# A transformer block in float32 on one core: the share of bands whose fourth convolution block runs on TensorE goes from 9 of 20 to 7 of 16, a norm group's two statistics become one step, and the order is computed anew

## The chip, the cores and the metric

The kernel runs on one core of a Trainium2 chip. The metric is device time in microseconds of one execution; the time before is the median of three runs. PE is TensorE, DVE is VectorE, ACT is ScalarE, POOL is GpSimd and SP is SyncE, which here only issues DMAs.

## The reference

For 16 images of 128 channels and 96x96 pixels, in float32 throughout: a norm over the channels of each pixel, channel attention with eight heads and a residual; a second norm, a feed-forward part of 512 hidden channels (1x1 in, 3x3 depthwise, exact GELU, 1x1 out) and a second residual.

```python
xn1 = _layernorm(x_hwc, ln1_w, ln1_b)
attn_out = _attention(xn1, wq, wk, wv, wp)
x = x + attn_out.transpose(0, 3, 1, 2)
xn2 = _layernorm(x_hwc, ln2_w, ln2_b).transpose(0, 3, 1, 2)
x = x + _ffn(xn2, w_in, w_dw, w_out)
# _attention: q, k normalised over the pixels; softmax(q k^T * scale) is 16x16 for each head
# _ffn:
h1 = jnp.einsum('bchw,oc->bohw', xn_nchw, w_in[:, :, 0, 0])
h2 = lax.conv_general_dilated(h1, w_dw, ..., padding=((1, 1), (1, 1)), feature_group_count=HID)
h3 = jax.nn.gelu(h2, approximate=False)
return jnp.einsum('bchw,oc->bohw', h3, w_out[:, :, 0, 0])
```

## The kernel before

**Tiling.** Channels lie on the 128 partitions. An image is cut into six *bands* of 16 rows (96 bands in all), a band into four *units* of 4 rows (384 pixels). The 512 hidden channels are four *blocks* of 128.

**The norms.** Each norm works on groups of 512 pixels, 18 to an image (288 groups for each norm, 576 in all). `forth` (L662) transposes the group on PE into one of two PSUM banks (`pT_a`, `pT_b` for the first and second norm), so that a pixel's channels lie along a row. `stats` (L669) takes the statistics on DVE, two instructions of 256 elements for a group. POOL makes the variance (`ve`, L676) and its power -1/2 (`rstd`, L680); for the second norm DVE makes one small vector (`nb`, L684). ACT scales the group out of PSUM (`zT`, L716 and L720), and PE transposes it back (`pB`, L767), whence ACT places it in a ring of rows in SBUF (`xn`, L771, L773). In the first norm PE also accumulates a Gram matrix from `zT` (L730), from which the attention is worked out.

**The feed-forward part.** For a band and a block, a *job*: PE multiplies by the input weights (`hidden`, L942, four matmuls), ACT copies the result into a padded buffer `h1` of the block (`kept`, L945). Of the nine taps of the 3x3 convolution, the centre and six others are taken on DVE (`tap`, L970): six instructions of some 1,520 elements, which accumulate in place in one `h3` buffer, the first from the centre row, each later one onto what the one before it wrote. The last two taps are products on ACT (`products`, L963), which two DMAs from POOL's queue add on (L977). ACT then applies GELU (L981). A job of the fourth block can be done by PE instead: `by_matmuls` (L1035) takes nine matmuls for each unit, 36 for the band, with combined weights `comp`, and ACT applies GELU to each unit straight from PSUM (L1041). There is then no `hidden`, no `kept`, no tap, no product and no DMA for that block. Which bands do so is told by `by_pe`. Last, PE multiplies by the output weights (`ffn_out`, L1059, four matmuls for a unit); ACT evicts the result (L1069) and a DMA adds it to the output; in the last two bands DVE adds it (L1066) and SP stores it.

**The order.** Nothing is ordered by hand. Each step is given to a planner (`Plan.op`) with its engine, a supposed duration, a place in the program, what it reads and writes, and the buffers it takes. `Plan.order` then runs a list schedule: at each moment an engine takes, of the steps that are ready and have buffers, the one with the lowest place. A place is the step's position in the sequence of jobs plus an offset from the table `AT`, one for each kind of step (a second one, with `_0`, for the start). `SLACK` makes results appear later to the planner than the work alone would, `T_ADD` and others are its supposed DMA costs. The planner's answer fixes the order of the instructions on every engine; each engine then runs its queue in that order and waits where a result is late. So a change of any of these numbers moves steps all over the program.

## Time and profile before

| | before |
|---|---|
| median of 3 runs (lowest, highest) | 4053.81 us (4053.22, 4065.76) |
| the profiled execution, its own time | 4053.42 us |
| its span, first to last instruction | 4051.7 us |
| PE busy | 4014.3 us, 99% |
| DVE busy | 3968.5 us, 98% |
| ACT busy | 3581.5 us, 88% |
| POOL busy | 2639.7 us, 65% |
| bytes moved by DMA | 829.49 MB, 205 GB/s |

The profiled execution lies 0.4 us under the median, so its rows can be used for the median as they stand. 1.7 us of its time lie outside the span.

A row of the page's groups gives line, engine, operation, what is written and read, shape and count, then the busy time of the group in us, the mean of one in ns, and the idle time of the engine just before them with what ended it. Two things have to be kept in mind. A float32 matmul of the program is two matmul rows in the trace (L1035 stands there 3294 times, and 1647 times in the program). And a row's duration holds the time in which the result still travels, while the next instruction has already begun: the pace of an engine is read from the distance between two starts.

### The profile page before, as it was taken

How to read it: one execution, taken by the hardware profiler on the slowest of the kernel's cores; microseconds unless marked ns; L12 is line 12 of the kernel's file. 1: busy time of each engine (PE TensorE's matmuls, PEld its weight loads, DVE VectorE, ACT ScalarE, POOL GpSimd, SP SyncE). 2: the span in 40 equal slices, each digit the busy share in tenths (PEclk: the TensorE clock that was granted, in tenths of full speed). 3: DMA queues.
4: the chain of work that ended last, by engine and by line, in shares of the span. 5: the costliest groups of instructions: out<-in, count | busy, mean ns of one | idle time of the engine just before them, and what ended most of it. 6: DMA issues, size and time to landing. Idle time of an engine off the chain costs nothing. (4 is left out here: it accounts for less than half of the span.)

```text
span 4051.7 us, 50785 instructions
## 1 busy us (share of the span) xinstructions
PE 4014.3 (99%) x17209; PEld 2631.2 (65%) x17209; DVE 3968.5 (98%) x3773; ACT 3581.5 (88%) x6678; POOL 2639.7 (65%) x2166
## 2 busy tenths in 40 slices
PE   8999999999999999999999999999999999999999
PEld 6666666666666666666666666666666666666665
DVE  7999999999999999999999999999999999999998
ACT  5989899998898989888989898989989998899974
POOL 4767667576775757757577575766757767576631
PEclk9999999999999999999999999999999999999999
DMA  5999899999999999999999999999999999999997
GB/s 141 209 190 227 181 216 212 213 218 189 217 221 206 219 183 229 208 202 218 189 223 202 204 226 192 221 203 203 225 200 218 210 217 212 190 220 197 213 177 149
DMA packets 196290, 829.49 MB, mean 205 GB/s; under 512 B 22720, under 2 KB 24256, under 8 KB 196032
## 3 DMA queue, kind: packets, MB, share of 16 engines
q0 software_dynamic: 138096, 674.43, 86.0%
q1 hardware_dynamic: 55584, 151.02, 10.4%
q8 instruction: 137, 2.24, 0.2%
q10 hardware_dynamic: 2352, 0.81, 0.1%
q14 instruction: 121, 0.99, 0.1%
HBM read 150.62 MB, written 149.42 MB: 74 GB/s over the span
## 5 line engine op out<-in xcount | busy, mean ns | idle before, releaser
L970 DVE SCALAR_TENSOR_TENSOR h<-h,ratio,h 128x1520 f32<-128x1520 f32 (+1 forms) x1697 | 2994.8, 1780 | 6.1
L1035 PE MATMUL h<-xn,comp 128*128 128x380 f32 (+3 forms) x3294 | 1143.7, 478 | 1.0 <-ACT h L945 1.0
L1059 PE MATMUL h<-h,woutT 128*128 128x384 f32 x3072 | 1133.3, 488 | 2.5 <-ACT h L945 1.6
L963 ACT ACTIVATE h<-h,ratio 128x1536 f32<-128x1536 f32 (+1 forms) x676 | 1090.9, 1624 | 7.4 <-PE h L1059 3.4
L942 PE MATMUL h<-xn,winT 128*128 128x384 f32 (+3 forms) x2698 | 1057.0, 494 | 1.2 <-ACT h L1041 1.1
L977 POOL DMA_DIRECT2D h<-h x676 | 628.2, 950 | 604.8 <-ACT h L963 245.4
L1035 PEld LDWEIGHTS h<-xn,comp 128*128 128x128 f32 x3294 | 595.2, 191 | 332.1 <-issue 16.5
L945 ACT COPY h<-h 128x384 f32<-128x384 f32 (+1 forms) x1307 | 670.2, 544 | 139.8 <-PE h L942 127.9
L1059 PEld LDWEIGHTS h<-h,woutT 128*128 128x128 f32 x3072 | 558.2, 191 | 336.1 <-issue 39.4
L942 PEld LDWEIGHTS h<-xn,winT 128*128 128x128 f32 x2698 | 487.1, 191 | 275.0 <-issue 19.3
L970 DVE SCALAR_TENSOR_TENSOR h<-h,ratio 128x1536 f32<-128x1536 f32 x339 | 614.3, 1813 | 7.8 <-ACT h L945 7.0
L680 POOL TENSOR_TENSOR rstd_a<-ve_a,mhalf 128x4 f32<-128x4 f32 x288 | 583.7, 2027 | 17.3
L680 POOL TENSOR_TENSOR rstd_b<-ve_b,mhalf 128x4 f32<-128x4 f32 x288 | 575.9, 2000 | 13.0
L676 POOL TENSOR_SCALAR ve_a<-st_a 128x4 f32<-128x4 f32 x288 | 364.6, 1266 | 282.5 <-DVE st_a L669 233.5
L981 ACT ACTIVATE h<-h 128x1536 f32<-128x1536 f32 x342 | 521.3, 1526 | 5.3 <-DVE h L970 3.4
L676 POOL TENSOR_SCALAR ve_b<-st_b 128x4 f32<-128x4 f32 x288 | 362.2, 1258 | 242.7 <-DVE st_b L669 210.8
L720 ACT ACTIVATE zT<-pT_b,nb_b,rstd_b 128x128 f32<-128x128 f32 x1132 | 436.3, 500 | 26.7 <-DVE nb_b L684 26.2
L716 ACT ACTIVATE zT<-pT_a,rstd_a 128x128 f32<-128x128 f32 x1080 | 320.1, 420 | 32.6 <-POOL rstd_a L680 31.9
L611 PE MATMUL h<-xn,mwT 128*128 128x384 f32 x768 | 296.3, 489 | 5.3 <-ACT x L620 1.4
L730 PEld LDWEIGHTS g<-zT 128*128 128x128 f32 x2160 | 272.4, 191 | 32.6
L730 PE MATMUL g<-zT 128*128 128x129 f32 x2160 | 285.5, 275 | 0.0
L771 ACT ACTIVATE xn<-pB_b,b 128x384 f32<-128x384 f32 x384 | 249.5, 650 | 19.4 <-PE pB_b L767 19.1
(175 smaller groups left out, 3471.4 us busy)
## 6 DMA issues: line engine op xcount, KB each, us to landing
h<-h POOLq DMA_DIRECT2D x564, 768.0 KB, 10.1
h<-h POOLq DMA_DIRECT2D x112, 720.0 KB, 13.4
x<-in_x_dram SPq DMA_DIRECT2D x192, 384.0 KB, 7.9
out_dram<-x SPq DMA_DIRECT2D x190, 384.0 KB, 9.9
x<-in_x_dram POOLq DMA_DIRECT2D x189, 384.0 KB, 9.9
out_dram<-h POOLq DMA_DIRECT2D x94, 768.0 KB, 11.2
out_dram<-x SPq DMA_DIRECT2D x4, 192.0 KB, 1.9
h<-in_L_conv_w_in_dram ACTq DMA_DIRECT2D x1, 256.0 KB, 6.0
```

Source lines behind the costliest of these rows:

```text
L676: nc.gpsimd.tensor_scalar(ve, d["mv"][:, :, 2], 1.0 / C, EPS, ALU.mult, ALU.add)
L680: nc.gpsimd.tensor_tensor(rstd, d["ve"], mhalf, ALU.pow)
L720: nc.scalar.activation(zT(q)[:, k, :P], d["pT", q][:, k, :], AF.Identity, bias=d["nb"][:, t : t + 1], scale=d["rstd"][:, t : t + 1],)
L730: nc.tensor.matmul(grams[i][:, : P + 1], lhsT=zt[:, :P], rhs=zt, start=(q == 0 and k == 0), stop=(q == NU * TPU // QT - 1 and k == QT - 1),)
L942: nc.tensor.matmul(rows(ph)[:, k : k + m, :], lhsT=winT[:, n, :], rhs=z, start=True, stop=True)
L945: nc.scalar.copy(window(h1_, r, e - r, 1), rows(d.pop(("ph", r))))
L963: nc.scalar.activation(d["pr", t][:, o0:o1, :], shifted(t, o0, o1), AF.Copy, scale=ratio[:, n, t : t + 1])
L970: nc.vector.scalar_tensor_tensor(h3[:, o0:o1, w0:w1], shifted(t, o0, o1, w0, w1), ratio[:, n, t : t + 1], onto, ALU.mult, ALU.add)
L977: nc.gpsimd.dma_start(out=to[:, o0:o1, :], in_=d["pr", t][:, o0:o1, :], accum_op=ALU.add)
L981: nc.scalar.activation(h3, h3, AF.Gelu)
L1035: nc.tensor.matmul(d["pc"][:, o0 + k : o0 + k + m, w0:w1], lhsT=comp[:, t, :], rhs=z[:, :, w0 + dx : w1 + dx], start=(t == order[0]), stop ...
L1059: nc.tensor.matmul(rows(d["po"]), lhsT=woutT[:, n, :], rhs=h3s[g, n][:, s * UR : (s + 1) * UR, :], start=(k == 0), stop=(k == NCH - 1),)
```

## The change

The share of bands, after the first six and before the last six, whose fourth block PE takes is 7 of 16 instead of 9 of 20. With the lists for the first and last image, which stay, this is 44 bands instead of 45. The two statistics of a group become one step of the planner, with one result instead of two: they stand next to each other on DVE, and the variance waits for the step as a whole. In the planner, a result of PE is taken as 360 ns late instead of 200, the adding DMAs as some 1% dearer, their issue as 800 ns instead of 1000, and `AT` has other offsets throughout (two of its lines are shown).

```diff
-PE_SHARE = (9, 20)
+PE_SHARE = [7, 16]
...
-    stats_a=-129.45, variance_a=101.85, power_a=12.15, scaled_a=-477.7, gram=7.8, back_a=-124.0, place_a=56.75,
+    stats_a=-149.6, variance_a=301.9, power_a=66.85, scaled_a=-439.7, gram=7.8, back_a=-93.85, place_a=-80.7,
...
-SLACK = dict(PE=200, DVE=0, ACT=100, POOL=0, ADD=800, MOVE=1020)
+SLACK = dict(PE=360, DVE=0, ACT=100, POOL=0, ADD=800, MOVE=1010)
...
-T_ADD, T_DRAM, T_MOVE = (68.9, 240.62), (15.9, 750), 125
+T_ADD, T_DRAM, T_MOVE = (69.55, 242.89), (16.05, 750), 125
...
-        op("POOL", 1000, p, f, r, w, 350 + SLACK["ADD"], late[1], T_ADD[0] + n * (T_ADD[1] + late[0]))
+        op("POOL", 800, p, f, r, w, 350 + SLACK["ADD"], late[1], T_ADD[0] + n * (T_ADD[1] + late[0]))
...
-            def stats(j):
+            def stats():
 
-                if j == 0:
-                    d["st"] = small.tile([P, QB * QT // 2, 6], F32, tag="st", name=f"st_{name}_{m}")
-                h, k = divmod(2 * j, QT)
-                nc.vector.bn_stats(
-                    d["st"][:, j, :], d["pT", qs[h]][:, k : k + 2, :].rearrange("p t c -> p c t")
-                )
+                d["st"] = small.tile([P, QB * QT // 2, 6], F32, tag="st", name=f"st_{name}_{m}")
+                for j in range(QB * QT // 2):
+                    h, k = divmod(2 * j, QT)
+                    nc.vector.bn_stats(
+                        d["st"][:, j, :], d["pT", qs[h]][:, k : k + 2, :].rearrange("p t c -> p c t")
+                    )
...
-            for j in range(QB * QT // 2):
-                dve(341, at("stats" + ab, s, i), lambda j=j: stats(j), [trs[2 * j // QT]], [(*bt, j)])
-            pool(T_VARIANCE, at("variance" + ab, s, i), variance, [(*bt, j) for j in range(QB * QT // 2)], [(*bt, "r")])
+            dve(341 * QB * QT // 2, at("stats" + ab, s, i), stats, trs, [(*bt, "s")])
+            pool(T_VARIANCE, at("variance" + ab, s, i), variance, [(*bt, "s")], [(*bt, "r")])
```

Counted over the whole program, the instructions that differ in number are these, and no others:

| | before | change |
|---|---|---|
| PE, conv matmuls (L1035) | 1647 | 1608 |
| PE, `hidden` matmuls (L942) | 1349 | 1353 |
| DVE, taps (L970) | 2036 | 2042 |
| ACT, products (L963) | 676 | 678 |
| ACT, copies of `kept` (L945), of `halo` (L937) | 1307, 247 | 1311, 249 |
| ACT, GELU of a job or a unit (L981, L1041) | 522 | 519 |
| POOL, adding DMAs (L977) | 676 | 678 |

(Three of the 39 conv matmuls are halves of units that the ring's end cut in two.) And this is how DVE's instructions follow each other:

| a DVE instruction and the next one | before | change |
|---|---|---|
| tap, then a tap onto the same `h3` buffer | 173 | 128 |
| tap, then a tap of another job | 704 | 1110 |
| tap, then a statistic | 969 | 516 |
| statistic, then a statistic | 164 | 615 |

The first place is DVE in the middle of the program, around the thirteenth group of the first norm of the eighth image (`st_a7_12`; `st_b6_14` is a group of the second norm of the image before it). A tap's row names the `h3` buffer it writes, the `h1` buffer it reads and, unless it is a job's first, the `h3` buffer again. Before:

```order
L669 BN_STATS st_a7_12_12175<-pT_a7_12_12167 128x6
L970 TENSOR_SCALAR h3_0_134<-h1_0_130,ratio_101,h3_0_134 128x16x95
L669 BN_STATS st_a7_12_12175<-pT_a7_12_12167 128x6
L970 TENSOR_SCALAR h3_9_143<-h1_1_131,ratio_101 128x1536
L970 TENSOR_SCALAR h3_9_143<-h1_1_131,ratio_101,h3_9_143 128x16x95
L669 BN_STATS st_b6_14_12219<-pT_b6_14_12208 128x6
L970 TENSOR_SCALAR h3_9_143<-h1_1_131,ratio_101,h3_9_143 128x16x95
L669 BN_STATS st_b6_14_12219<-pT_b6_14_12208 128x6
L970 TENSOR_SCALAR h3_9_143<-h1_1_131,ratio_101,h3_9_143 128x16x95
L669 BN_STATS st_a7_13_12256<-pT_a7_13_12245 128x6
```

The same place in the change:

```order
L670 BN_STATS st_a7_12_12175<-pT_a7_12_12167 128x6 x2
L970 TENSOR_SCALAR h3_12_146<-h1_0_130,ratio_101,h3_12_146 128x16x95
L970 TENSOR_SCALAR h3_10_144<-h1_1_131,ratio_101,h3_10_144 128x16x95 x2
L670 BN_STATS st_b6_14_12225<-pT_b6_14_12211 128x6 x2
L970 TENSOR_SCALAR h3_10_144<-h1_1_131,ratio_101,h3_10_144 128x16x95
L970 TENSOR_SCALAR h3_4_138<-h1_2_132,ratio_101 128x1536
L970 TENSOR_SCALAR h3_10_144<-h1_1_131,ratio_101,h3_10_144 128x16x95
L670 BN_STATS st_a7_13_12270<-pT_a7_13_12251 128x6 x2
```

The single statistics that stood between the taps of one job have drawn together in pairs, and taps of two jobs alternate where a statistic stood.

The second place is the end of the program on PE: the convolution of the last unit, and the first of the 28 output matmuls (L1059) that follow it. Before:

```order
L1059 MATMUL h_77<-h_2_136,woutT 128x384
L1035 MATMUL h_79<-xn,comp 128x384
L1035 MATMUL h_79<-xn,comp 128x4x95
L1035 MATMUL h_79<-xn,comp 128x384
L1035 MATMUL h_79<-xn,comp 128x4x95 x3
L1035 MATMUL h_79<-xn,comp 128x3x95
L1035 MATMUL h_79<-xn,comp 128x288
L1035 MATMUL h_79<-xn,comp 128x3x95
L1059 MATMUL h_78<-h_11_145,woutT 128x384
```

In the change:

```order
L1059 MATMUL h_76<-h_9_143,woutT 128x384
L1035 MATMUL h_78<-xn,comp 128x384
L1035 MATMUL h_78<-xn,comp 128x4x95
L1035 MATMUL h_78<-xn,comp 128x384
L1035 MATMUL h_78<-xn,comp 128x4x95 x3
L1035 MATMUL h_78<-xn,comp 128x3x95
L1035 MATMUL h_78<-xn,comp 128x288
L1035 MATMUL h_78<-xn,comp 128x3x95
L1059 MATMUL h_79<-h_5_139,woutT 128x384
```

Only the buffers are others: the end of PE's work is the same, and the last 28 output matmuls stand behind the last convolution in both.

More of the change, by code (lines that the diff above doesn't have):

```diff
@@ L39 @@
 AT = dict(
-    load_1=82.6, load_2=-78.35, tables=-212.55, weights=-8.7, zeros=-1.95, load_a=-129.65, forth_a=-4.4,
-    stats_a=-129.45, variance_a=101.85, power_a=12.15, scaled_a=-477.7, gram=7.8, back_a=-124.0, place_a=56.75,
-    attention=-133.5, mix=-2.85, residual=-61.35, mixed=-62.7, add_x=-136.1, forth_b=-9.5, stats_b=-264.05,
-    variance_b=-172.85, power_b=-141.85, shift_b=-73.95, scaled_b=-122.75, back_b=-102.05, place_b=206.65,
-    evicted=-16.5, add_out=78.2, halo=32.25, hidden=4.7, kept=-206.45, products=422.15, add_last=-37.85,
@@ L45 @@
-    tap=75.4, add_first=-297.3, gelu=100.85, conv=3.75, conv_gelu=-145.15, out=8.15, add=82.8, store=-128.45,
-    mix_0=-136.0, residual_0=73.7, mixed_0=111.0, add_x_0=110.9, gram_0=8.3, forth_a_0=-45.35, forth_b_0=-8.35,
-    stats_a_0=-127.4, stats_b_0=-132.2, scaled_a_0=-123.55, scaled_b_0=125.95, back_a_0=20.8, back_b_0=-144.95,
-    place_a_0=195.95, place_b_0=185.85, shift_b_0=-26.1, late=-92.4, store_x2=44.5, store_x2_0=65.3,
-    variance_a_0=-154.25, variance_b_0=103.25, power_a_0=-134.5, power_b_0=22.95, attention_0=-151.75,
@@ L50 @@
-    load_a_0=-180.2, hidden_0=4.5, kept_0=101.75, products_0=611.4, tap_0=9.4, add_last_0=-60.45,
-    add_first_0=-65.9, gelu_0=522.55, conv_0=2.55, conv_gelu_0=-134.2, out_0=7.1, evicted_0=-324.5,
+    load_1=17.15, load_2=132.15, tables=-22.4, weights=-91.85, zeros=10.0, load_a=-138.25, forth_a=-4.4,
+    stats_a=-149.6, variance_a=301.9, power_a=66.85, scaled_a=-439.7, gram=7.8, back_a=-93.85, place_a=-80.7,
+    attention=-134.3, mix=-2.85, residual=-430.5, mixed=-76.2, add_x=28.5, forth_b=-9.5, stats_b=-430.85,
@@ new lines @@
+    variance_b=4.45, power_b=-337.6, shift_b=-147.05, scaled_b=-135.45, back_b=-27.9, place_b=208.6,
+    evicted=116.2, add_out=-44.8, halo=62.6, hidden=4.7, kept=-434.0, products=278.95, add_last=25.1, tap=162.8,
+    add_first=-73.6, gelu=137.4, conv=3.75, conv_gelu=-292.35, out=8.15, add=-67.45, store=-63.15,
+    mix_0=-136.35, residual_0=89.15, mixed_0=158.7, add_x_0=67.7, gram_0=-70.45, forth_a_0=-133.4,
+    forth_b_0=-8.3, stats_a_0=603.95, stats_b_0=31.65, scaled_a_0=202.2, scaled_b_0=166.1, back_a_0=21.15,
@@ L52 @@
+    back_b_0=-342.5, place_a_0=-173.65, place_b_0=-83.55, shift_b_0=-105.35, late=2.4, store_x2=-72.15,
+    store_x2_0=-47.15, variance_a_0=-97.7, variance_b_0=160.4, power_a_0=16.3, power_b_0=44.75,
+    attention_0=-415.8, load_a_0=-461.9, hidden_0=4.6, kept_0=57.85, products_0=793.75, tap_0=91.6,
+    add_last_0=-39.0, add_first_0=91.05, gelu_0=102.7, conv_0=2.75, conv_gelu_0=-130.25, out_0=6.5,
+    evicted_0=233.4,
 )
 STEP = dict(scaled=0.3, hidden=0.1, products=0.5, tap=0.166, conv=1.6, conv_tap=0.03, out=0.8, out_part=0.05)
-SLACK = dict(PE=200, DVE=0, ACT=100, POOL=0, ADD=800, MOVE=1020)
+SLACK = dict(PE=360, DVE=0, ACT=100, POOL=0, ADD=800, MOVE=1010)
```

## The prediction

> **What bounds the kernel now.** I cut the span at 78 us, where DVE's first tap starts, and at 4034 us, where its last one ends; a view by stretches gives each engine's busy time in us with its instructions, then PE's granted clock, the DMA engines' share and GB/s:

> ```profile
> 0.00:78.00 78.00, 63.94 (x405) 51.45 (x406) 48.30 (x164) 33.50 (x88) 34.28 (x92) 1.00 0.44 124
> 78.00:4034.00 3956.00, 3936.24 (x16762) 2571.79 (x16761) 3916.61 (x3604) 3545.02 (x6587) 2605.40 (x2076) 1.00 0.98 207
> 4034.00:4052.00 18.00, 14.14 (x44) 8.00 (x42) 3.62 (x7) 2.98 (x5) 0.00 (x0) 0.99 0.22 87
> ```

> The order is PE, weight loads, DVE, ACT, POOL. In the 3956 us between the cuts PE lacks 19.8 us of being always busy and DVE 39.4. Two engines stand at their limit, so neither alone tells what a shift of work from one to the other is worth: what it adds to DVE counts in full unless DVE's idle time shrinks. That time, by what ended it (us in total, times, longest):

> ```profile
> DVE h L970 <- ACT h L945: 7.0, 9, 2.3
> DVE nb_b L684 <- POOL rstd_b L680: 7.0, 8, 1.2
> DVE st_a L669 <- PE pT_a L662: 6.5, 17, 0.7
> DVE st_b L669 <- PE pT_b L662: 5.4, 14, 1.3
> DVE n L865 <- PE g L859: 1.2, 1, 1.2
> DVE h L970 <- PE h L1059: 0.7, 1, 0.7
> ...
> ACT h L945 <- PE h L942: 127.3, 251, 2.5
> ```

> PE itself ends 13.8 us of it (6.5 + 5.4 + 1.2 + 0.7). The copies of `kept` end 7.0 more, and the last row, from ACT's waits, shows that these copies are themselves late because of PE. So 20.8 us stem from PE and 7.0 from POOL's power.

> Last, the end of the program, PE and then DVE:

> ```profile
> 4029.91 18.22 PE L1059 MATMUL h<-h,woutT 128*128 128x384 f32 x56
> ...
> 4026.76 7.04 DVE L970 SCALAR_TENSOR_TENSOR h<-h,ratio,h 128x1425 f32<-128x1425 f32 x4
> 4048.17 0.56 DVE L1066 TENSOR_TENSOR x<-h,x 128x384 f32<-128x384 f32 x1 [2.02 <-PE h L1059]
> ```

> The last tap ends at 4033.8. PE's last 56 rows run without a gap up to 4048.1, so PE is behind there, if only a little.

> **PE's part.** Pieces of the chain of waits show PE's pace (start, us, what):

> ```profile
> 3142.85 2.58 PE h L942 x8
> ...
> 3886.07 8.97 PE h L1035 x28
> ```

> A row of the convolution takes 8.97 / 28 = 0.320 us, one of `hidden` 2.58 / 8 = 0.3225. The fourth block of one band leaves PE: 36 matmuls are 72 rows, 23.1 us; four `hidden` matmuls, 8 rows, come, 2.6 us. PE has **20.5 us** less to do.

> **DVE's part.** One job more is six taps. Their pace:

> ```profile
> 1258.63 1.81 DVE L970 SCALAR_TENSOR_TENSOR h<-h,ratio 128x1536 f32<-128x1536 f32 x1
> 1260.36 10.36 DVE L970 SCALAR_TENSOR_TENSOR h<-h,ratio,h 128x1520 f32<-128x1520 f32 x6
> 1270.63 1.81 DVE L970 SCALAR_TENSOR_TENSOR h<-h,ratio 128x1536 f32<-128x1536 f32 x1
> ```

> From start to start a first tap takes 1.73 and a later one (1270.63 - 1260.36) / 6 = 1.71: 1.73 + 5 x 1.71 = **+10.3 us**.

> The order changes the price of the others. The next rows are two taps onto one `h3` buffer, two taps of different jobs, and a tap with a statistic on either side:

> ```profile
> 1103.38 3.63 DVE L970 SCALAR_TENSOR_TENSOR h<-h,ratio,h 128x1520 f32<-128x1520 f32 x2
> 1106.93 0.43 DVE L669 BATCH_NORM_STATS2 st_b<-pT_b 128x6 f32<-128x256 f32 x1
> ...
> 1398.55 3.51 DVE L970 SCALAR_TENSOR_TENSOR h<-h,ratio,h 128x1520 f32<-128x1520 f32 x2
> 1401.98 0.43 DVE L669 BATCH_NORM_STATS2 st_a<-pT_a 128x6 f32<-128x256 f32 x1
> 1402.32 1.79 DVE L970 SCALAR_TENSOR_TENSOR h<-h,ratio,h 128x1520 f32<-128x1520 f32 x1
> 1404.02 0.43 DVE L669 BATCH_NORM_STATS2 st_a<-pT_a 128x6 f32<-128x256 f32 x1
> ```

> The first pair needs 3.55 us up to the next start, the second 3.43: a tap that continues what the one before it wrote costs 0.12 us more. Such pairs fall from 173 to 128: 45 x 0.12 = **-5.4 us**. A tap before a statistic takes 1.70 (1404.02 - 1402.32), 0.01 less than before a tap of another job; the latter pairs grow by 406, **+4.1 us**. DVE's work grows by 10.3 - 5.4 + 4.1 = **9.0 us**.

> [...]

> **What other work hides.** ACT gets two products, four copies and a GELU, and loses four GELUs of units:

> ```profile
> L963 ACT ACTIVATE h<-h,ratio 128x1536 f32<-128x1536 f32 x564 | 919.4, 1639 | 7.3 <-PE h L1059 3.4
> L981 ACT ACTIVATE h<-h 128x1536 f32<-128x1536 f32 x338 | 519.6, 1538 | 2.0 <-DMA h<-h 1.6 <-DVE h L970 0.2
> L945 ACT COPY h<-h 128x384 f32<-128x384 f32 x1040 | 519.2, 532 | 98.8 <-PE h L942 91.6 <-DVE h L970 3.2 <-PE h L1059 1.0
> L1041 ACT ACTIVATE h<-h 128x384 f32<-128x384 f32 x180 | 95.6, 531 | 111.9 <-PE h L1035 111.4
> ```

> That is 3.3 + 2.1 + 1.5 - 2.1 = 4.8 us, and under 1.1 for two more halo copies, which are shorter than those of `kept`. ACT is idle for 411 us of the stretch, so I count nothing; without this cover it would be about 6. Two adding DMAs join POOL's queue:

> ```profile
> q0 software_dynamic: 138096, 674.43, 86.0%
> ...
> h<-h POOLq DMA_DIRECT2D x564, 768.0 KB, 10.1
> ```

> 86.0% of the span is 3484 us for 674.43 MB, so 4.1 us for 768 KB and 8.1 for both. The engines' share is 0.98, which leaves some 79 us, and GELU waited only 1.6 us for these DMAs (the L981 row): nothing counted, 8 if the cover is gone. The job's two products also hold two of the 15 `h3` buffers for a while; a tap that waits for a buffer would wait for the output matmuls that read it last, which is 0.7 us in the list of DVE's waits: nothing counted. SP's instructions keep their number; loads and stores of `x` are reordered with the rest, within that same share.

> **Where idle time can go.** Of the 20.8 us that stem from PE, between none and all can end, since PE gets 20.5 us free. I take 14: freed time doesn't all fall where a wait is. Of POOL's 7.0, between none and all: two statistics side by side let the variance begin one tap, 1.7 us, earlier wherever a tap stood between. I take 5. At the end the four units of the last band must follow the last tap, and four times eight rows of 0.3225 are 10.3 us of the 14.3 between 4033.8 and 4048.1; PE's lag is the other 4, of which I take 2. The start, whose order also changes, I leave as it is. The new order can also bring idle time; its nearest row is DVE's 39.4 us, and as much again is the outer bound.

> The sum, on the profiled execution's 4053.4 us (0.4 under the median): 4053.4 + 9.0 - 14 - 5 - 2 = **4041 us**.

> **The rivals.** *PE sets the pace.* Its busy share is the higher, and the chain of waits is almost all PE:

> ```profile
> PE 22%; DVE 2%; ACT 1%; POOL 1%; issue 0%; POOLq 0%; DVEq 0%; ACTq 0%
> ...
> L1035 PE MATMUL h<-xn,comp 128*128 128x380 f32 (+3 forms) x3294 | 1143.7, 478 | 1.0 <-ACT h L945 1.0
> ```

> Then all 20.5 us come off: **4033**. DVE's idle time would have to fall from 39.4 to 39.4 - 9.0 - 20.5 = 9.9 us. Against it: PE's busy time contains ends that are only travel, 478 ns a row for L1035 where the pace is 320, so PE is less full than it looks.

> *DVE sets the pace and its waits stay.* The six rows hold 50 waits, none over 2.3 us, 17 of them in the largest group: so they look like waits that come from an order and not from load. Then 4053.4 + 9.0 = **4062**.

> *Taps shut POOL out.* A variance that begins inside a tap lasts until that tap ends, and the power likewise:

> ```profile
> 1404.36 3.51 DVE L970 SCALAR_TENSOR_TENSOR h<-h,ratio,h 128x1520 f32<-128x1520 f32 x2
> ...
> 1404.55 1.66 POOL L676 TENSOR_SCALAR ve_a<-st_a 128x4 f32<-128x4 f32 x1 [0.70 <-DVE st_a L669]
> 1406.29 2.47 POOL L680 TENSOR_TENSOR rstd_a<-ve_a,mhalf 128x4 f32<-128x4 f32 x1
> ```

> The first tap of the pair ends at about 1406.1 and the variance at 1406.2. Tap after tap rises from 877 to 1238 pairs, so fewer statistics leave POOL a gap, and `rstd` comes later. Today 8 of 288 `nb` wait 0.9 us each; if 25 did, that is 15 us more on DVE and **4077**. It decides from some 13 late `nb` upward, if nothing is won elsewhere. Against it: the pairs begin the chain earlier. [...]

> **How the numbers follow.** 0.3%, 12 us, is about what a measurement of this kernel can tell from no change; the three runs differ by as much. The forecast gets 0.45, PE's pace 0.17, the waits that stay 0.21, POOL 0.17. Faster than 4041.6 is half of the first and all of the second, 0.40; slower than 4066 is POOL's case and a fifth of the third, 0.21; 0.39 lies between. The forecast's own range is 4034 to 4050. The whole range, 4024 to 4072, holds PE's case with the start a few us better, the waits that stay, and the milder half of POOL's; left out are about 0.05 below and 0.13 above.

> **What would show it.** Between first and last tap: DVE's listed waits near 9 us, not 28; PE's busy time some 20 us lower; pairs still 3.63 and 3.51. After the last tap 16 us, not 18. If the waits are again 28 the third case holds; if `nb` waits are 20 or more, the fourth. The forecast is wrong if DVE's waits at PE don't fall although PE has 20 us less to do.

## The result, and the profile after

The change takes **4074.85 us** (median of 6 runs, 4072.61 to 4077.75), the kernel before on the same chip 4056.34 (6 runs): **1.0044 times as long, 95% interval 1.0031 to 1.0057**. The forecast was 4041 with a range of 4024 to 4072. The profiled execution of the change took 4074.26 us, its span 4072.5.

The view by stretches, cut at the first tap's start and at the last tap's end as before (PE, weight loads, DVE, ACT, POOL, then PE's granted clock):

```profile
0.00:79.00 79.00, 65.14 (x402) 53.60 (x403) 46.76 (x159) 32.83 (x87) 32.85 (x89) 0.94 0.42 117
79.00:4057.00 3978.00, 3935.13 (x16702) 2558.78 (x16701) 3925.14 (x3614) 3550.47 (x6593) 2670.15 (x2080) 1.00 0.98 206
4057.00:4072.50 15.50, 11.96 (x38) 6.70 (x36) 3.54 (x7) 2.95 (x5) 0.00 (x0) 0.97 0.23 89
```

Against before, the start is 1 us longer, the middle 22 (3978 for 3956), the end 2.2 shorter (15.5 for 17.7): the span's 20.8. In the middle DVE's busy time grew by 8.5 us (3925.14 for 3916.61; 9.2 if one cuts at the very taps) and **its idle time by 13.5, from 39.4 to 52.9**. PE's idle time more than doubled, from 19.8 to 42.9, and its busy time fell by 1 us only, though it has 20.5 us less to do. What ended the waits (us in total, times, longest), of DVE:

```profile
DVE st_b L670 <- PE pT_b L663: 12.5, 25, 1.4
DVE nb_b L685 <- POOL rstd_b L681: 12.4, 15, 1.5
DVE st_a L670 <- PE pT_a L663: 9.0, 17, 1.6
DVE h L970 <- ACT h L945: 4.9, 7, 1.3
DVE h L970 <- PE h L1059: 2.1, 2, 1.5
```

The two waits for PE's transposes are 21.5 us, where before they were 11.9; POOL's power 12.4 for 7.0; only the copies of `kept` fell, 4.9 for 7.0. And of PE:

```profile
PE pB_b L767 <- ACT xn L771: 7.0, 9, 2.6
PE pT_b L663 <- ACT zT L717: 6.9, 7, 2.2
PE h L1059 <- ACT h L945: 5.5, 5, 2.3
PE pT_a L663 <- ACT zT L717: 4.4, 7, 1.2
PE g L853 <- DVE wide L846: 3.3, 1, 3.3
```

PE waits for ACT, which scales and places what the norms made. How such a wait goes round can be read from one place in the timeline (start, length, what, in brackets the idle time before and what ended it), left to a few rows:

```profile
2125.39 3.62 DVE L970 SCALAR_TENSOR_TENSOR h<-h,ratio,h 128x1520 f32<-128x1520 f32 x2
2125.39 2.67 POOL L681 TENSOR_TENSOR rstd_a<-ve_a,mhalf 128x4 f32<-128x4 f32 x1
...
2128.10 1.14 ACT L717 ACTIVATE zT<-pT_a,rstd_a 128x128 f32<-128x128 f32 x4 [3.76 <-POOL rstd_a L681]
...
2129.30 1.11 PE L663 MATMUL pT_b<-ident,x 128*128 128x128 f32 x4 [2.24 <-ACT zT L717]
...
2130.45 0.76 DVE L670 BATCH_NORM_STATS2 st_b<-pT_b 128x6 f32<-128x256 f32 x2 [1.44 <-PE pT_b L663]
...
2136.20 0.76 DVE L670 BATCH_NORM_STATS2 st_a<-pT_a 128x6 f32<-128x256 f32 x2 [1.56 <-PE pT_a L663]
```

POOL's power runs into DVE's second tap, ACT's scaling waits for it with everything queued behind, PE can't transpose the next group before the scaling has emptied a bank, and DVE's next statistics come 1.44 us late. So at this place one late result is paid by all four engines in turn. The four transposes at 2129.30 take 1.11 us; at 2123.30 the same took 0.60. PE's clock has just gone to half, and that is told of next.

PE's granted clock is at one half for four spells in the middle of the change, 6.8 us from 1818.7, 3.4 from 2129.3, 6.8 from 2487.7 and 6.8 from 3825.7; before there was one of 3.4 us at 2071.9. PE around the first and ahead of the last:

```profile
1814.70 0.44 PE L767 MATMUL pB_b<-ident,zT 128*128 128x128 f32 x2 [0.45 <-ACT xn L771]
1816.54 0.33 PE L767 MATMUL pB_b<-ident,zT 128*128 128x128 f32 x1 [1.41 <-ACT zT L721]
1819.43 0.90 PE L767 MATMUL pB_b<-ident,zT 128*128 128x128 f32 x3 [2.56 <-ACT xn L771]
1821.58 2.93 PE L1059 MATMUL h<-h,woutT 128*128 128x384 f32 x4 [1.24 <-ACT h L945]
...
3823.56 0.55 PE L767 MATMUL pB_b<-ident,zT 128*128 128x128 f32 x3 [0.30 <-ACT xn L771]
3825.49 0.75 PE L767 MATMUL pB_b<-ident,zT 128*128 128x128 f32 x3 [1.39 <-ACT xn L771]
```

Each spell comes right behind waits of one to three microseconds. The four stretches around them (the number behind POOL's is the clock):

```profile
1800.00:1830.00 30.00, 23.50 (x92) 14.67 (x91) 29.24 (x33) 23.87 (x45) 20.22 (x17) 0.89 1.05 223
2120.00:2140.00 20.00, 17.76 (x81) 12.24 (x80) 16.93 (x18) 14.50 (x35) 15.38 (x12) 0.91 0.91 201
2480.00:2500.00 20.00, 16.33 (x66) 11.12 (x65) 19.59 (x22) 10.46 (x19) 9.80 (x7) 0.83 0.95 197
3815.00:3835.00 20.00, 16.02 (x61) 10.09 (x60) 19.06 (x20) 17.97 (x35) 16.54 (x12) 0.83 1.06 224
```

30 x 0.11 + 20 x (0.09 + 0.17 + 0.17) = 11.9 us of PE's work lost, 1.7 before: half of the 20.5 us that the change frees on PE.

The end is shorter by 2.7 us, where 2 were forecast:

```profile
4050.73 18.22 PE L1059 MATMUL h<-h,woutT 128*128 128x384 f32 x56
...
4055.58 1.71 DVE L970 SCALAR_TENSOR_TENSOR h<-h,ratio,h 128x1440 f32<-128x1440 f32 x1
```

The last tap ends at 4057.3, 15.2 us before the span's end; 17.9 before.

### The profile page after: what moved, and what is told of

Read it like the earlier page. It is cut to its first block, busy times and chain, and to the rows that moved or that the text cites. A ratio compares the mean times of both kernels' runs of the same rounds, so it can differ in the third digit from the quotient of the medians.

```text
span 4072.5 us, 50779 instructions
## 1 busy us (share of the span) xinstructions
PE 4012.2 (99%) x17139; PEld 2619.1 (64%) x17139; DVE 3975.5 (98%) x3779; ACT 3586.2 (88%) x6683; POOL 2703.0 (66%) x2168
## 3 DMA queue, kind: packets, MB, share of 16 engines
q1 hardware_dynamic: 55584, 151.02, 10.3%
## 5 line engine op out<-in xcount | busy, mean ns | idle before, releaser
L970 DVE SCALAR_TENSOR_TENSOR h<-h,ratio,h 128x1520 f32<-128x1520 f32 (+2 forms) x1702 | 2973.7, 1778 | 4.5
L1059 PE MATMUL h<-h,woutT 128*128 128x384 f32 x3072 | 1135.3, 489 | 5.8 <-ACT h L945 5.5
L1035 PE MATMUL h<-xn,comp 128*128 128x380 f32 (+5 forms) x3216 | 1119.8, 478 | 1.8 <-ACT h L945 1.1
L963 ACT ACTIVATE h<-h,ratio 128x1536 f32<-128x1536 f32 (+1 forms) x678 | 1099.1, 1634 | 7.6 <-PE h L1059 3.3
L942 PE MATMUL h<-xn,winT 128*128 128x384 f32 (+2 forms) x2706 | 1059.1, 493 | 1.3 <-ACT x L621 0.8
L977 POOL DMA_DIRECT2D h<-h x678 | 632.9, 963 | 606.7 <-ACT h L963 274.9
L945 ACT COPY h<-h 128x384 f32<-128x384 f32 (+1 forms) x1311 | 683.2, 558 | 145.7 <-PE h L942 131.9
L1035 PEld LDWEIGHTS h<-xn,comp 128*128 128x128 f32 x3216 | 579.2, 190 | 324.8 <-issue 21.2
L1059 PEld LDWEIGHTS h<-h,woutT 128*128 128x128 f32 x3072 | 557.9, 191 | 340.6 <-issue 38.5
L942 PEld LDWEIGHTS h<-xn,winT 128*128 128x128 f32 x2706 | 485.5, 190 | 270.8 <-issue 20.9
L970 DVE SCALAR_TENSOR_TENSOR h<-h,ratio 128x1536 f32<-128x1536 f32 x340 | 615.1, 1809 | 7.9 <-ACT h L945 4.9
L681 POOL TENSOR_TENSOR rstd_a<-ve_a,mhalf 128x4 f32<-128x4 f32 x288 | 596.0, 2070 | 15.0
L677 POOL TENSOR_SCALAR ve_a<-st_a 128x4 f32<-128x4 f32 x288 | 398.2, 1383 | 235.7 <-DVE st_a L670 205.5
L981 ACT ACTIVATE h<-h 128x1536 f32<-128x1536 f32 (+1 forms) x343 | 525.6, 1534 | 11.7 <-DMA h<-h 11.3
L677 POOL TENSOR_SCALAR ve_b<-st_b 128x4 f32<-128x4 f32 x288 | 391.5, 1360 | 201.9 <-DVE st_b L670 186.1
## 6 DMA issues: line engine op xcount, KB each, us to landing
h<-h POOLq DMA_DIRECT2D x566, 768.0 KB, 10.2
h<-h POOLq DMA_DIRECT2D x112, 720.0 KB, 13.5
x<-in_x_dram POOLq DMA_DIRECT2D x189, 384.0 KB, 10.6
out_dram<-h POOLq DMA_DIRECT2D x94, 768.0 KB, 11.2
```

Of the source, the lines that this page charges most:

```text
L677: nc.gpsimd.tensor_scalar(ve, d["mv"][:, :, 2], 1.0 / C, EPS, ALU.mult, ALU.add)
L681: nc.gpsimd.tensor_tensor(rstd, d["ve"], mhalf, ALU.pow)
L942: nc.tensor.matmul(rows(ph)[:, k : k + m, :], lhsT=winT[:, n, :], rhs=z, start=True, stop=True)
L945: nc.scalar.copy(window(h1_, r, e - r, 1), rows(d.pop(("ph", r))))
L963: nc.scalar.activation(d["pr", t][:, o0:o1, :], shifted(t, o0, o1), AF.Copy, scale=ratio[:, n, t : t + 1])
L970: nc.vector.scalar_tensor_tensor(h3[:, o0:o1, w0:w1], shifted(t, o0, o1, w0, w1), ratio[:, n, t : t + 1], onto, ALU.mult, ALU.add)
```

## The experiments

Line numbers of the experiments shift by a few against the change. Times are medians, ratios stand against the kernel before on the same chip. Work and idle time of DVE are those between the first tap's start and the last tap's end.

**The load without the order.** First the change's loads were put into the order of before, which stays as it is. e1 leaves out the last matmul of the last unit in 32 of the 45 bands, so a ninth of that unit's convolution is missing there; e2 does five taps, one in every sixtieth job, twice, so that their products are in the sum twice; e3 does both.

```diff
+        kth = pe_bands.index(g)
+        light = s == UPB - 1 and (kth + 1) * 32 // 45 > kth * 32 // 45
...
+            if light and t == order[-1]:
+                return
```
```diff
+            for _ in range(2 if j % 60 == 40 and t == left[3] else 1):
                 nc.vector.scalar_tensor_tensor(
```

> The order of before, with one convolution matmul of 32 bands left out (the last tap of the band's last unit, so that term is missing from the sum): 32 x 0.64 = 20.5 us less for PE, as in the change, and nothing else. Against before at 4056. The prediction's step (PE's freed time ends two thirds of the waits that stem from PE, 14 us, and 2 at the end): 4040. PE alone sets the pace: 4036. DVE sets the pace and its waits come from the order: at most the 2 to 4 us at the end, 4052 to 4056, with the waits of DVE on PE still above 15 us.

> The order of before, with five taps done twice (one in every sixtieth job, so those sums are wrong): 5 x 1.83 = 9.2 us more for DVE, the net load that the change brings. DVE sets the pace: 4065, all 9.2. PE alone sets the pace: 4056. Both by turns: about 4060.

> Both of these edits: the load of the change in the order of before (one term of 32 units left out, five taps done twice). The prediction's step with the order held: +9.2 - 14 - 2, 4049. DVE sets the pace whatever PE does: 4062 to 4065. If this is at or under before while the change is 18.5 over it, the order and not the load is to blame for the 18.5; if it is 4065, half of the 18.5 is load.

Measured: e1 4047.31 us (ratio 0.9985, 0.9974 to 0.9996), e2 4060.92 (1.0012, 1.0004 to 1.0021), e3 4057.89 (1.0009, 0.9996 to 1.0023). e1's waits of DVE:

```profile
DVE nb_b L684 <- POOL rstd_b L680: 7.9, 10, 1.2
DVE h L970 <- ACT h L945: 5.5, 8, 2.1
DVE st_a L669 <- PE pT_a L662: 3.8, 9, 0.7
DVE st_b L669 <- PE pT_b L662: 3.4, 9, 1.3
```

PE's 20.5 us bring 7 us, a third. With 1.2 more for one wait at `g`, the waits that stem from PE are 13.9 us, 20.8 before; all of DVE's idle time falls from 39.4 to 33.7. That is 6 to 7 us where 14 were forecast. DVE's added taps cost 7. Only 2.6 us of PE's freed time show as idle time of PE (22.4 for 19.8); its busy time fell by 10.6 of the 20.5, so the rows that are left last some 10 us longer in all. Together the loads cost some 4 us, with an interval from 2 us less to 9 more. By subtraction the order owes the rest of the 18.5, some 15.

**The merged statistics in the old order.** e4 moves the first statistic of each group down to the place of the second and leaves every other instruction where it was. So there are more taps onto the buffer of the tap before (394 for 173) and more next to a tap of another job (874 for 704).

```diff
-                h, k = divmod(2 * j, QT)
-                nc.vector.bn_stats(
+                for j in range(QB * QT // 2) if j else ():
+                    h, k = divmod(2 * j, QT)
+                    nc.vector.bn_stats(
```

> The order of before, with each group's first statistic moved down to the second: the merged step without a new schedule. Pairs of taps onto one buffer rise from 173 to 394 and pairs of different jobs from 704 to 874. By the prices of the prediction DVE has 221 x 0.12 + 170 x 0.01 = 28 us more: 4084 if all of it is paid. If merging by itself shuts POOL out, DVE's waits for the power rise well over 7 us and the time over 4090. If a pair onto one buffer costs nothing extra, 4056.

Measured: 4094.68 us (1.0097, 1.0080 to 1.0114). DVE's work grew by 22 us and its idle time by 20, where the two prices of the prediction give 28. The prices are met by the 22 and a part of the 20: a tap's row lasts some 1.79 us; the next tap of another job starts 1.71 after its start, some 0.08 ahead of the row's end, and the next one onto the same buffer 1.83 after it. So some 0.035 of the 0.12 is a gap between two rows, which counts as idle time. Such gaps hold 14.3 us here and 6.1 before, 8 more. Most of the other idle time is the wait for the power:

```profile
DVE nb_b L685 <- POOL rstd_b L681: 24.9, 61, 1.2
```

Merging alone, in an order that doesn't know of it, is dear on both counts: 394 pairs onto one buffer instead of 173, and 61 late `nb` instead of 8. The change's new order spares most of this (15 late `nb`).

**The parts, each with a new order.** e5 to e8 take the parts of the change apart, and the planner computes an order for each.

```diff
-PE_SHARE = (9, 20)
+PE_SHARE = [7, 16]
```

That is e5. e6 is the kernel before with the merged step alone, e7 with both, e8 the change with 9 of 20 put back.

> The kernel before with the share of 7 of 16 and nothing else; the order is computed from its own offsets. Its shift of load, in the old order, was worth some +4 us in the run e3. Theory A (the share is the cause): within 5 us of the change's 4075. Theory B (the merged step is the cause) and theory C (the offsets of the change suit this chip less than the old ones): near the kernel before, 4054 to 4062. Theory D (the order as a whole: any recomputed order leaves other coincidences of late results, and the old one was a good draw): anywhere from 4050 to 4095, and the time goes with DVE's idle time between first and last tap (39 us before, 53 in the change).

> The kernel before with the two statistics of a group as one step and nothing else; the order is computed from its own offsets. The counts of instructions are those of before. Theory A: 4050 to 4060. Theory B: near 4075, with waits at POOL's power near the change's 12.4 us or more. Theory C: near 4055. Theory D: 4050 to 4095, along with DVE's idle time.

> The kernel before with the share of 7 of 16 and the merged step, but the old offsets, slack and costs of the planner: it differs from the change in these numbers alone. Theories A and B: near 4075. Theory C: near 4058 (before plus the load's 4). Theory D: 4050 to 4095, along with DVE's idle time; if it is well over the change, then the change's offsets are better for its content than the old ones, and C falls.

> The change with the old share of 9 of 20, so with the instruction counts of before, and the change's offsets and merged step. Theory A: near 4056. Theories B and C: 4070 to 4075. Theory D: 4050 to 4095, along with DVE's idle time.

**Nothing but another order.** e9 and e10 change one offset of the kernel before by 0.05, e11 and e12 the same offsets of the change.

```diff
-... gelu=100.85, conv=3.75, conv_gelu=-145.15, out=8.15, ...
+... gelu=100.85, conv=3.7, conv_gelu=-145.15, out=8.15, ...
```

> The kernel before with one offset of the planner 0.05 lower (conv 3.70 for 3.75): the work, the share, the two separate statistics and every other number stay, only the order is computed anew. If the loss of the change needs the change's share, step or numbers, this one stays at 4050 to 4060. Theory D: 4065 to 4090, as the four runs before it (4074 to 4083), with DVE's idle time between first and last tap at 50 us or more instead of 39.

> The kernel before with another offset a little changed (out 8.20 for 8.15), all else as it was. Same two forecasts as for e9: 4050 to 4060 if the cause is in the change's own parts, 4065 to 4090 by theory D, by which the kernel before is one fortunate order among its near neighbours.

> The change with its offset conv 0.05 lower (3.70 for 3.75), all else as in the change. If the change's parts cause the loss: 4072 to 4078 again. Theory D: somewhere from 4065 to 4095; over 4075 if the change's order too is one of the better of its neighbours.

> The change with its offset out 0.05 higher (8.20 for 8.15), all else as in the change. Same forecasts as for e11. All of e9 to e12 together: by theory D their times follow DVE's idle time plus its work, not the share or the step; kernels with the same content lie as far from each other as before and change (18.5 us).

Measured, with the two kernels of the study (half clock: PE's time at half the clock in the middle of the program; work and idle time are those of the one profiled execution of each):

| | share, step, offsets | time, us | ratio | DVE work | DVE idle | PE idle | half clock |
|---|---|---|---|---|---|---|---|
| before | old, old, old | 4052 to 4056 | 1 | 3916.2 | 39.4 | 19.8 | 3.4 |
| e9 | old, old, old, conv 3.70 | 4067.35 | 1.0035 (1.0022 to 1.0048) | 3918.6 | 47.0 | 27.2 | 3.4 |
| e10 | old, old, old, out 8.20 | 4081.55 | 1.0066 (1.0051 to 1.0081) | 3920.2 | 62.6 | 33.1 | 27.3 |
| e5 | new, old, old | 4083.25 | 1.0074 (1.0059 to 1.0089) | 3923.4 | 64.8 | 53.1 | 23.9 |
| e6 | old, new, old | 4080.01 | 1.0067 (1.0052 to 1.0082) | 3920.2 | 61.5 | 36.5 | 10.2 |
| e7 | new, new, old | 4082.30 | 1.0071 (1.0056 to 1.0086) | 3924.9 | 55.9 | 50.8 | 10.2 |
| e8 | old, new, new | 4074.04 | 1.0053 (1.0036 to 1.0069) | 3921.5 | 54.9 | 33.3 | 10.2 |
| change | new, new, new | 4074.85 | 1.0044 (1.0031 to 1.0057) | 3925.4 | 52.8 | 42.9 | 23.9 |
| e12 | new, new, new, out 8.20 | 4086.91 | 1.0086 (1.0069 to 1.0103) | 3929.7 | 56.3 | 55.2 | 20.5 |
| e11 | new, new, new, conv 3.70 | 4113.87 | 1.0150 (1.0135 to 1.0165) | 3928.8 | 89.5 | 69.7 | 58.0 |

Theories A and B fall: e5 without the merged step and e6 without the new share are both slower than the change, and e10, with neither, is slower too. Theory C falls with e7, which has the old offsets and is not faster than the change. D holds: all nine orders computed anew are slower than the kernel before, by 0.35 to 1.5% or 15 to 62 us, whatever they contain, and DVE's idle time makes about half of it or more. Two of its forecasts were missed all the same: e9 has 47.0 us of idle time where 50 or more were named, and e11 lies beyond 4095. e8 alone would have suited B and C. e10 does the very work of before and has 23.2 us more of DVE's idle time; its waits:

```profile
DVE st_b L669 <- PE pT_b L662: 16.1, 18, 2.8
DVE st_a L669 <- PE pT_a L662: 14.3, 16, 3.0
```

Two kernels of the same content lie 14 us apart (e9, e10) or some 43 (the change and e11, each taken against before on its own chip). An effect of the share or of the step of its own below that can't be told from these runs, and A, B and C fall only as explanations of the whole loss.

**The half clock.** e13 puts empty matmuls ahead of the instructions that wait before the four spells; e14 puts as many elsewhere. They write to a free part of a bank, and nothing reads them.

```diff
+                    warm(kind, c, j)
                     nc.tensor.transpose(d["pB"][:, j * P : (j + 1) * P], zTs[q][:, k, :P], ident)
```

> The change, with 87 empty matmuls of 128x128 (0.11 us each, 9.5 us in all) put ahead of the instructions at which PE waits just before its four spells at half clock (about 1815, 2127, 2485 and 3825 us); order and all else as in the change. The spells last 23.8 us and so cost PE 11.9 us of work. Theory H (the half clock is a cost of its own, which the waits bring about): the four spells vanish, the granted clock rises from 0.996 to 0.998 or 0.999, and the time falls by 6 to 12 us, to 4063 to 4069. Theory I (the spells are only a sign, the time lies in the waits of the order): the time stays within 3 us of the change's 4075, whatever the clock does.

> The change with the same 87 empty matmuls, but put some tens of us earlier (in the attention of another image for 25 of them), where PE doesn't wait before a spell: what 9.5 us more of work on PE costs by itself. Theory H: the spells stay, 4075 to 4085. Theory I: 4075 to 4085 as well; if this one falls like e13, the filling as such and not its place is what helps.

Measured: e13 4069.60 us (1.0037, 1.0024 to 1.0050), e14 4089.02 (1.0086, 1.0071 to 1.0101). The dose was larger than meant: 62 of the 87 are two rows each in the trace and so take 0.22 us, 16.4 us in all. e13's stretches around the same places, some us earlier:

```profile
1800.00:1830.00 30.00, 29.16 (x163) 21.79 (x162) 30.00 (x31) 25.04 (x47) 20.82 (x18) 1.00 1.05 223
2118.00:2138.00 20.00, 20.00 (x116) 15.21 (x115) 17.56 (x18) 15.18 (x36) 15.52 (x13) 1.00 0.93 209
2474.00:2494.00 20.00, 19.21 (x103) 13.77 (x102) 19.90 (x23) 13.46 (x26) 8.94 (x6) 1.00 0.99 202
3812.00:3832.00 20.00, 17.64 (x80) 12.06 (x79) 18.98 (x20) 17.68 (x33) 16.73 (x11) 0.91 1.06 224
```

Three spells are gone, and the last is 3.4 us instead of 6.8, behind another wait that had not been filled. PE has 16.4 us **more** to do, and the program is 14.6 us slower than before on its chip where the change is 18.5: some 4 us are won, though the two intervals overlap. Between first and last tap of the profiled executions it is 5.2 us (3973.0 for 3978.2), 4.4 of them DVE's idle time. The same matmuls where PE doesn't wait before a spell (e14, same chip as e13) leave four spells and are 19 us slower than e13, some 15 slower than the change and 4 beyond what was expected. So the sign is theory H's, the half clock costs of itself, but less than forecast, and e13's time alone is hardly outside the 3 us that theory I allows.

> The change with empty matmuls ahead of the same waits, but about half as many (42 of 0.22 us and 25 of 0.11 us, 12 us in all, none longer than its wait), and 9 of them also ahead of the output matmul that waited 2.1 us before the spell that e13 left. If the half clock is a cost of its own: no spell in the middle, and 2 to 5 us less than e13's 4069.6, so 4064 to 4068. If e13's gain was already all of it: 4068 to 4071.

With the matmuls fitted to the waits: 4066.88 us (1.0034, 1.0022 to 1.0046), one spell of 3.4 us. Between first and last tap it takes 3973.1 us, as e13 does; what it has over e13 lies in the start, which is 2.2 us shorter, and so isn't the dose's. Over before on its chip it is 13.9 us slower, so it wins 4.6 of the 18.5 and confirms e13. With the filling itself in it, the half clock's price is 4 to 5 us.

> The kernel before with 13 empty matmuls (0.22 us each) ahead of the two waits of 0.85 and 1.83 us that precede its one spell of 3.4 us at 2072 us. The spell costs PE 1.7 us of work; by e13's rate (5 us for 10.2 us of PE's work) that is 0.8 us, at most 1.7: 4052 to 4055, too little to be told from the kernel before by the interval, though the spell should be gone from the trace.

```diff
+        for _ in range({("back_b", 197, 1): 4, ("forth_b", 150): 1, ("forth_b", 151): 8}.get(at, 0)):
```

Measured: 4055.60 us (1.0003, 0.9994 to 1.0012). The spell at 2072 is gone, another of 3.4 us stands at 3456 of the profiled execution, and nothing is won. No kernel that does all the work came out below the kernel before.

**PE's load in the change's order.** e15 takes 32 conv matmuls out of the change, as e1 did of before (the same ninth of a unit is missing).

> The change with another 32 matmuls of the convolution left out (64 rows of 0.320 us, 20.5 us less for PE; the last tap of the last unit is missing in 32 bands), the order as it is. In the old order the same edit brought 6 to 7 us (run e1). If PE's load has a part in the change's waits: 4060 to 4068, with the waits at pT down from 22 us to 15 or less. If they come from the order alone: 4070 to 4076, PE's idle time up by some 20 us.

Measured: 4066.56 us (1.0028, 1.0017 to 1.0039), 11.6 us over before on its chip where the change is 18.5: 7 us for 20.5 us of PE's work. Its waits for the transposes:

```profile
DVE st_b L670 <- PE pT_b L663: 9.3, 19, 1.5
DVE st_a L670 <- PE pT_a L663: 7.9, 19, 0.8
```

They fall from 21.5 to 17.2 us: more than none, and not to 15. Load has a part in the waits, the smaller one.

## Why the prediction was wrong

**DVE's work** was to grow by 9.0 us: it grew by 9.2, cut at the very taps. The prices are right: from start to start, a tap of 1,520 elements takes 1.83 us before one onto the same buffer and 1.71 before one of another job, in the change as in the kernel before, and e4 bears them out. That the sum is so close is luck in part. By kind of instruction the taps took 11.1 us more (a part of the saving on pairs is idle time, not work), the statistics 3.9 less (one before a tap takes 0.33 us where it follows another statistic, 0.34 where it stands alone) and the small vectors 2.0 more; the last two stand in no term.

**The tail** was to give 2 us and gave 2.7, but not, or not mainly, by PE's load: with the same share the time after the last tap is 17.4 to 18.0 us in e5, e7, e11 and e12 and 15.2 in the change, and e1, with the load alone, has 16.6 for 17.9. **The start** was left as it is and took 0.9 more. **POOL and ACT** hid nearly all that they were to hide: in DVE's list stands one wait of 0.3 us for an adding DMA and none for a product, though GELU's own waits for these DMAs on ACT rose from 1.6 to 11.3 us, 5.4 of them in one wait at the very end.

**The step that failed is "Where idle time can go".** It took 14 us off for PE and 5 for POOL, and put nothing on for the new order, although it named 39.4 us more as the outer bound. In the place of -19 stands +13.5. Three things are in it.

The first is a term that was mis-sized: what 20.5 us of PE's time are worth. Two thirds of the waits that stem from PE were to end, 14 us. e1 and e15 measured 6 us off DVE's idle time in either order, and 7 off the time. The prediction had the reason at hand and used it only for its third rival: short waits, spread over the program, look like an order's, not a load's.

The second is that the waits belong to the order. The old order is a good one among its neighbours, by fortune or because its offsets were searched for, which nothing here tells: a nudge of 0.05 in one offset gives 7.6 or 23.2 us more of DVE's idle time with the same work. The change has 13.5 more, and is among the better of the orders computed anew. A diff that moves every offset had to be read as a new draw, with a loss as the likeliest, and not as the old order with a few us shifted. The merged step was to spare POOL's waits 5 us; they grew by 5.4, to 15 late `nb`, and there are 18 and 22 in e12 and e11. That there are 13 and 11 in e5 and e10, without the step, and 8 and 6 in e6 and e7, with it, shows that the order rather than the step sets their number; what the step of its own adds to them stays open.

The third is the half clock, 24 us of it instead of 3.4, which the waits on PE bring about. It gave back half of what PE was relieved of. e13, which takes away 17 of the 24 us, has 4.4 us less of DVE's idle time, so the half clock costs some 4 to 5 of the 13.5; the other 9 are left to the order by subtraction.

**The rivals.** The times of the third, 4062, and of the fourth, 4077, stand on either side of the result, but neither is what happened. The third wanted the old waits of 28 us to stay; the rows of listed waits have 44 now. The fourth wanted 20 late `nb` or more and got 15, just over the 13 from which it was to decide, and POOL's part is 5.4 us of the 20.8. The sign that the prediction named for its own fall is the one that came: DVE's waits at PE didn't fall although PE has 20 us less to do. Its other sign, PE's busy time some 20 us lower, failed too: half clock stretches the rows by some 10 us, and in e1, without it, 20.5 us less work lowered the busy time by 10.6 only.

What stays open: which of the thousands of moved steps makes one order wait 39 us and its neighbour 63, and whether the share or the step has a small effect of its own. Separate statistics with the change's offsets weren't measured, with either share: for these the planner finds no order with the buffers that there are. Nor was a third resource near its limit tested: the DMA engines are 0.98 busy in the middle in both kernels, and in e1, where PE has less to do, GELU's waits for the adding DMAs are 21.1 us. How much of PE's freed time is lost there is open.

## What to carry to other kernels

Where a planner fixes the order on engines that are each some 98% busy, nudge a number that means nothing before the change is credited or blamed: here that alone moves the time by some 15 to 43 us, more than the loads of the change (4 us). Time freed on one of two engines at their limit came back only by a third (7 us for 20.5, in e1 and e15). And on TensorE, 99% busy in the middle, waits of some two microseconds were paid for twice, once as waits and once as half clock: 4 to 5 us for 24 us of half clock in the change, nothing that could be measured for the 3.4 us of before.

## What the runs showed of the hardware

And a power on POOL could last longer than two taps: in the change the row at 2113.82 lasts 4.07 us, inside four taps that follow each other without a wait (the variance before it, 3.27 us from 2112.08, still lasts when it begins), and one at 2129.29, where DVE stood still, 1.03 us.
